# Four column-quarter matmuls of a state sum, recorded as one operation of a planned kernel

## The chip, the core and the metric

The kernel runs on one core of a Trainium2 chip. The metric is the device time of one execution in microseconds, taken as the median of several runs. One execution was also recorded by the hardware profiler; its instructions, waits and DMA packets are what the views below are made of.

## What is computed

The input is 4 sequences of 1024 tokens with 256 features, in f32 throughout. Four parts follow each other, each in a normalised residual form, `x = x + layernorm(part(layernorm(x)))`:

1. an encoder of 4 layers (linear attention with 16 heads, then a feed-forward part 256 to 1024 to 256),
2. a gated low-rank layer,
3. a state-space layer, over chunks of 512 tokens: projections, a short convolution, and then, for 512 channels with 16 states each, the recurrence

```
h = h * dA + (d * u) * b          # for every channel and state, along the tokens
y = sum over states of h * c      # the state sum
```

4. eight experts, each token sent to one of them, each expert with room for 320 tokens.

The change concerns the last line of part 3, the sum over states.

## The kernel before

**Blocks.** The 4096 tokens are 8 blocks of 512 (`NBLK`), and block `j` is half `j % 2` of a sequence. The encoder runs over units (sequence, layer, block) in a software pipeline. The state-space layer runs over the blocks: `front(j)` makes projections and the step sizes and stores them to memory, `scan(j)` does the recurrence and the state sum, `back(j)` projects and normalises, `route(j)` chooses experts. `experts` runs the expert matmuls, beside scans 6 and 7.

**The scan.** A chunk of 128 partitions holds 16 channels of 8 states, so a block of 128 channels (`db`, four of them) is 8 groups, and 16 states are two halves (`k` = 0 and 1, `NSH` = 2). The groups are visited as two rounds (`r`) of four quarters (`q`). For each `(q, k)` of a round: DMAs bring the step sizes (`dd`), GpSimd multiplies them with `b` (`dbu`), ScalarE makes the decay into PSUM (`h`), VectorE runs `tensor_tensor_scan` in place and then multiplies with `c` into a tile `hc`. There are 8 buffers for `hc`, as many as one round makes. In the blocks 0 to 4 GpSimd adds the two halves (`hc` of `k` = 1 takes the sum), so that only that one is summed by TensorE; in the blocks 5 to 7 both are.

**The state sum.** `sums(tiles, r, k)` issues four matmuls, one for each quarter `q`: the stationary operand is a 128x32 matrix of ones (`gsum`), the moving one is the 128x512 `hc` of that quarter, and the output is a quarter of the 128 partitions of the PSUM tile `y`. `y` has one buffer. The sums of a round are recorded one after the first tiles of the round that follows (list `late`), or at the end of `db`. At the end VectorE reads `y` into `ys` and the next `db` begins. Over the kernel there are 5x4x2 + 3x4x2x2 = 88 such calls, or 352 matmuls.

**The planner.** Nothing is emitted in the order of the program text. Every call is recorded as an operation (`record`, then `add`) with its buffers, a time for which it holds its engine (`busy`) and a time to its result (`done`). `order` is a list scheduler: of all operations whose inputs are ready and whose buffers can be placed, it takes the one that can start first by these costs, and at equal times the one recorded first. It also hands out the buffers: a tile's buffer comes free when its last user has been placed in the order. The result is one fixed order for each engine; on the chip every engine works through its own order and waits where an input isn't there. The cost that `record` gives to a TensorE matmul is

```
busy = 0.877 * n if out.shape[0] == 32 else 1.754 * max(n, 64) + (34 if n < P else 4)
```

so a quarter of a state sum (32 output rows, `n` = 512) is planned at 449 ns, and four of them at 1796 ns.

How much scan work is recorded between two pieces of the encoder is set by `pump` with `SSM_RATE`, and by fixed costs in the generators; none of this depends on the planner's costs.

All of this is recorded through a helper, so that nearly every instruction in the profile has line 203; groups are told apart by the names of their tiles.

Of the kernel before, what the change touches and what calls it, by code (L numbers as in the profile page):

```python
# [39 lines left out]
NSH = N_STATE // SH  # L40
# [4 lines left out]
GQ = 32 // GC  # L45
# [101 lines left out]
OVERLAP = {"vector": 84, "scalar": 99, "gpsimd": 42}  # L147
HANDOVER = 36
ISSUE, SCATTER, FIND = 350, 1700, 1500

LANES = 8
LATENCY, LANDING, BYTES_PER_NS = 1300, 700, 270.0
# [10 lines left out]
def columns(x):  # L163
    return math.prod(x.shape[1:])


class Program:
# [23 lines left out]
    def record(self, engine, name, args, kwargs):  # L191
        out = kwargs["out"] if "out" in kwargs else args[0]
        outs = [out] + [kwargs[k] for k in ("accum_out",) if k in kwargs]
        every = list(args) + list(kwargs.values())
        ins = [a for a in every if a is not out and (isinstance(a, View) or hasattr(a, "tensor"))]
        if kwargs.get("start") is False:
            ins.append(out)

        def emit():
            def put(a):  # L200
                return a.place() if isinstance(a, View) else a

            getattr(getattr(self.nc, engine), name)(  # L203
                *map(put, args), **{k: put(v) for k, v in kwargs.items()}
            )

        n, load = columns(out), 0
        if "dma" in name:
            src = kwargs["in_"] if "in_" in kwargs else args[1]
            small = out if isinstance(out, View) else src  # L210
            load = 4 * math.prod(small.shape) / BYTES_PER_NS
            busy = done = ISSUE
        elif name == "transpose":
            busy, done = 0.877 * n + 22, 320
        elif engine == "tensor":
            done = 1.754 * n + 190
            busy = 0.877 * n if out.shape[0] == 32 else 1.754 * max(n, 64) + (34 if n < P else 4)
        else:
            table = {"vector": VECTOR_NS, "scalar": SCALAR_NS, "gpsimd": GPSIMD_NS}[engine]
            a, b = table[name]  # L220
            if name in ("tensor_reduce", "bn_stats"):
                n = columns(ins[0])
            done = a + b * n
            if engine == "scalar":
                done += 60 * sum(isinstance(kwargs.get(k), View) for k in ("scale", "bias", "accum_out"))
            busy = max(done - OVERLAP[engine], 50)
        return self.add(engine, emit, outs, ins, busy, done, load)

    def add(self, engine, emit, outs, ins, busy, done, load=0):
        op = Op(engine, emit, outs, ins, busy, done, load)  # L230
        before = set()
        for write, aps in ((False, ins), (True, outs)):
            for a in aps:
                self.access(op, a, write, before)
        before.discard(op)
        for b in before:
            b.after.append(op)
        op.before = len(before)
        op.rank = len(self.ops)
        self.ops.append(op)  # L240
        return op
# [119 lines left out]
    def emit(self):  # L361
        with self.tc.manual_schedule():
            for op in self.order():
                op.emit()
        self.reset()
# [21 lines left out]
def sandwich_kernel(ctx: ExitStack, tc: tile.TileContext, io: dict):  # L387
    nc = tc.nc
    x_in, out = io["x"], io["out"]
# [37 lines left out]
    nc = Program(tc)  # L427
# [121 lines left out]
    def layers(ctx: ExitStack):  # L549
# [436 lines left out]
        m = {}  # L986
# [176 lines left out]
        def scan(j):  # L1163

            half = j % NB
            BC = []
            for side in range(2):
                t = fpool.tile([P, NSH, TB], F32, tag=f"bc{side}", name=f"bc{side}")
                nc.sync.dma_start(
                    t, bcd[j][side].unsqueeze(0).to_broadcast([GC, SH, NSH, TB])  # L1170
                )
                BC.append(t)
            Bt, Ct = BC
            begun.append(j)
            ys = Y[j] = fpool.tile([P, NDB, TB], F32, tag="ys", name="ys")
            for db in range(NDB):
                y = ps_y.tile([P, TB], F32, tag="y", name="y")

                def sums(tiles, r, k):
                    for q in range(4):  # L1180
                        nc.tensor.matmul(
                            y[q * 32 : (q + 1) * 32, :],
                            m["gsum"][:, r, :],
                            tiles[q, k],
                            start=r == 0 and k == first[r],
                            stop=r == GQ - 1 and k == NSH - 1,
                        )


                first = [NSH - 1 if j < NBLK - 3 else 0 for r in range(GQ)]  # L1190

                late = []
                for r in range(GQ):
                    if r == GQ // 2:
                        xl = fpool.tile([P, TB], F32, tag="xl", name="xl")
                        nc.sync.dma_start(xl, xcd[j][db])
                        zl = fpool.tile([P, TB], F32, tag="zl", name="zl")
                        nc.sync.dma_start(zl, zsd[j][db])
                    tiles = {}
                    for q in range(4):  # L1200
                        g = q * GQ + r
                        gg = db * (P // GC) + g
                        dd = []
                        for k in range(2):
                            t = spool.tile([P, TB], F32, tag=f"dd{k}", name=f"dd{k}", bufs=3)
                            nc.sync.dma_start(
                                t,
                                dud[j][db][g * GC : (g + 1) * GC, k, :].unsqueeze(1).to_broadcast([GC, SH, TB]),
                            )
                            dd.append(t)  # L1210
                        for k in range(NSH):
                            dbu = spool.tile([P, TB], F32, tag="dbu", name="dbu", bufs=3)
                            nc.gpsimd.tensor_tensor(dbu, dd[1], Bt[:, k, :], ALU.mult)
                            h = ps_h.tile([P, TB], F32, tag="h", name="h")
                            nc.scalar.activation(
                                h, dd[0], AF.Exp, scale=m["A"][:, gg, k : k + 1]
                            )
                            last = m["last_h"][:, gg, k : k + 1]
                            nc.vector.tensor_tensor_scan(
                                h, h, dbu, 0.0 if half == 0 else last, ALU.mult, ALU.add  # L1220
                            )
                            if half < NB - 1:
                                nc.vector.tensor_copy(last, h[:, TB - 1 : TB])
                            hc = tiles[q, k] = spool.tile([P, TB], F32, tag="hc", name="hc", bufs=8)
                            nc.vector.tensor_tensor(hc, h, Ct[:, k, :], ALU.mult)
                            if late:
                                sums(*late.pop(0))
                        if first[r]:
                            nc.gpsimd.tensor_tensor(hc, tiles[q, 0], hc, ALU.add)
                        yield 4  # L1230
                    late = [(tiles, r, k) for k in range(first[r], NSH)]
                for args in late:
                    sums(*args)
                t = ys[:, db, :]
                nc.vector.scalar_tensor_tensor(
                    t, xl, m["mcol"][:, db, M_D : M_D + 1], y, ALU.mult, ALU.add
                )
                nc.gpsimd.tensor_tensor(t, t, zl, ALU.mult)
                yield 0.8
# [586 lines left out]
```

## Time and profile before

| | us |
|---|---|
| median of 3 runs | 2791.13 (2789.11 to 2801.9) |
| the profiled execution, its time | 2787.44 |
| the profiled execution, its span from first to last instruction | 2785.7 |
| PE (TensorE matmul) busy | 2378.6 (85%) |
| DVE (VectorE) busy | 1752.6 (63%) |
| ACT (ScalarE) busy | 1591.2 (57%) |
| POOL (GpSimd) busy | 1527.6 (55%) |
| mean granted TensorE clock | 0.92 |

PE is matmul time, PEld the loading of stationary operands, which overlaps it. A matmul of f32 stands in the records as two, so a matmul of the program is two records ("x2"), and one state sum of four quarters is eight. Busy time of a group of records is the time in which at least one of them runs; records that run at the same time count once. The granted clock (PEclk) is a share of full speed. A wait is named as waiter and releaser: "PE y <- DVE hc" is TensorE idle ahead of a `y` matmul until a VectorE instruction that writes `hc` has ended. The chain of waits is the chain of work that ended last, followed backwards.

The execution has four stretches. Up to about 800 us there is only the encoder. From there to about 1890 us the encoder runs beside the scans 0 to 3. To about 2320 us its last units run beside the scans 4 and 5; about 100 us without a scan follow, in which the last encoder block is finished and projected. From 2420 us the scans 6 and 7 run beside the experts, and the last block is finished.

### The profile page before, as it was taken

What the parts mean: (1) busy time and instruction counts of PE and PEld (TensorE: products, weight loads), DVE (VectorE), ACT (ScalarE), POOL (GpSimd) and SP (SyncE); (2) the same over time, 40 slices, a digit from 0 to 9 for tenths busy, and PEclk for the clock granted to TensorE, in tenths of its full rate; (3) what the DMA queues carried; (4) which work ended last, traced back from release to release, by engine and by line L of the source; (5) the groups of instructions that cost most, each with busy time, mean ns of one, the idle gap of its engine ahead of it and who ended that gap; (6) DMA issues with size and microseconds to landing.
All of it is one profiled execution on the core that took longest, in us unless ns stands there. A gap on an engine that the chain in (4) does not pass through costs nothing.

```text
span 2785.7 us, 29116 instructions
## 1 busy us (share of the span) xinstructions
PE 2378.6 (85%) x8308; PEld 1380.3 (50%) x8308; DVE 1752.6 (63%) x3291; ACT 1591.2 (57%) x3309; POOL 1527.6 (55%) x2005
## 2 busy tenths in 40 slices
PE   4889699998999999997989899986986975799776
PEld 2555456655555555555645555643443543344343
DVE  2121232223468878884449978896897894599895
ACT  4434454456676666664666766765665543666443
POOL 1101020123267667784429769885894773467774
PEclk8989899999999999999999999997897886899788
DMA  4011101112254344442245445445344352767762
GB/s 106 22 47 59 59 25 35 54 51 79 95 167 134 118 143 140 148 126 87 84 143 171 135 133 188 159 144 167 126 153 152 117 168 73 234 200 231 206 172 61
DMA packets 202218, 342.01 MB, mean 123 GB/s; under 512 B 32198, under 2 KB 79515, under 8 KB 198977
## 3 DMA queue, kind: packets, MB, share of 16 engines
q1 hardware_dynamic: 197760, 334.80, 38.3%
q0 software_dynamic: 4288, 5.27, 1.0%
q8 instruction: 68, 1.11, 0.2%
q14 instruction: 102, 0.83, 0.1%
HBM read 281.13 MB, written 59.92 MB: 122 GB/s over the span
## 4 chain that ended last, share of the span: by engine, by line
PE 41%; DVE 20%; POOL 14%; ACT 14%; issue 8%; DMA 3%; SPq 0%; POOLq 0%; DVEq 0%; ACTq 0%
PE mm L203 36%; DVE h L203 7%; ACT tok L203 6%; POOL dbu L203 5%; DVE hc L203 3%; PE kv L203 2%; PE y L203 2%; POOL tok L203 2%; POOL hc L203 2%; DVE st L203 2%; DVE xc L203 2%; POOL t L203 2%; ACT h L203 2%; DVE kv L203 1%; ACT t L203 1%
## 5 line engine op out<-in xcount | busy, mean ns | idle before, releaser
L203 POOL TENSOR_TENSOR dbu<-dd,bc 128x512 f32<-128x512 f32 x512 | 663.0, 1333 | 147.8 <-DVE h L203 104.5
L203 ACT ACTIVATE h<-dd,A 128x512 f32<-128x512 f32 x512 | 344.8, 687 | 317.7 <-DVE hc L203 304.1
L203 PE MATMUL mm<-w,fT 128*128 128x256 f32 x2176 | 486.6, 381 | 6.1 <-ACT t L203 2.7
L203 PEld LDWEIGHTS mm<-w,fT 128*128 128x128 f32 x2176 | 410.2, 190 | 86.6 <-issue 18.9
L203 DVE TENSOR_TENSOR_SCAN h<-h,last_h,dbu 128x512 f32<-128x512 f32 x256 | 321.6, 1279 | 62.2 <-ACT h L203 40.3
L203 DVE TENSOR_TENSOR hc<-h,bc 128x512 f32<-128x512 f32 x512 | 341.6, 678 | 9.8 <-PE y L203 8.1
L203 DVE TENSOR_TENSOR_SCAN h<-h,dbu 128x512 f32<-128x512 f32 x256 | 305.6, 1219 | 42.9 <-ACT h L203 33.0
L203 PE MATMUL y<-hc,gsum 128*32 128x512 f32 x704 | 222.2, 664 | 84.0 <-DVE hc L203 57.6
L203 PE MATMUL mm<-hT,w1a 128*128 128x512 f32 (+1 forms) x576 | 269.0, 617 | 14.8 <-ACT hT L203 11.0
L203 PE MATMUL mm<-hT,w1b 128*128 128x512 f32 (+1 forms) x576 | 251.2, 583 | 12.8 <-ACT fT L203 6.2
L203 POOL TENSOR_TENSOR hc<-hc,hc 128x512 f32<-128x512 f32 x160 | 213.8, 1336 | 52.6 <-DVE hc L203 46.8
L203 PE MATMUL mm<-wkv,hT 128*128 128x512 f32 x512 | 228.2, 597 | 1.5 <-ACT xi L203 0.8
L203 ACT ACTIVATE fT<-mm,cols 128x512 f32<-128x512 f32 x256 | 170.8, 682 | 85.5 <-PE mm L203 84.8
L203 PE MATMUL mm<-ident,tok 128*128 128x128 f32 x696 | 114.0, 306 | 107.9 <-ACT tok L203 105.9
L203 POOL TENSOR_SCALAR ve<-mv 128x4 f32<-128x4 f32 (+1 forms) x105 | 20.7, 197 | 335.1 <-DVE mv L203 323.0
L203 DVE TENSOR_TENSOR X<-X,mm 128x512 f32<-128x512 f32 x128 | 86.7, 679 | 169.8 <-PE mm L203 169.5
L203 POOL TENSOR_TENSOR X<-X,ro 128x1024 f32<-128x1024 f32 x64 | 151.3, 2367 | 68.3 <-ACT tok L203 48.4
L203 PEld LDWEIGHTS mm<-hT,w1a 128*128 128x128 f32 x576 | 113.0, 205 | 147.9 <-issue 97.6
L203 PEld LDWEIGHTS mm<-hT,w1b 128*128 128x128 f32 x576 | 107.5, 191 | 152.2 <-issue 102.4
L203 ACT ACTIVATE tok<-X,nb,rs 128x256 f32<-128x256 f32 x288 | 149.3, 589 | 43.3 <-POOL nb L203 42.7
L203 PEld LDWEIGHTS mm<-ident,tok 128*128 128x128 f32 x696 | 86.6, 154 | 164.6 <-ACT tok L203 127.7
L203 ACT ACTIVATE tok<-tok,nb,rs 128x256 f32<-128x256 f32 x252 | 131.3, 589 | 60.8 <-POOL nb L203 58.4
(194 smaller groups left out, 3925.6 us busy)
## 6 DMA issues: line engine op xcount, KB each, us to landing
dd<-dud SPq DMA_DIRECT2D x512, 256.0 KB
w<-in_w_dram SPq DMA_DIRECT2D x16, 1024.0 KB
dud<-t SPq DMA_DIRECT2D x32, 512.0 KB
tok<-in_x_dram SPq DMA_DIRECT2D x16, 512.0 KB
wkv<-in_wkv_dram SPq DMA_DIRECT2D x16, 512.0 KB
w1a<-in_w_dram SPq DMA_DIRECT2D x16, 512.0 KB
w1b<-in_w_dram SPq DMA_DIRECT2D x16, 512.0 KB
t<-in_w_in_dram SPq DMA_DIRECT2D x16, 512.0 KB
```

What stands on the lines that cost most here:

```text
L203: getattr(getattr(self.nc, engine), name)(*map(put, args), **{k: put(v) for k, v in kwargs.items()})
```

## The change

The four matmuls of a call of `sums` become one operation for the planner, which emits them one behind the other. The operation has all four quarters as inputs, so it is placed when all four `hc` tiles are ready, and their buffers come free together, when it is done. Its planned cost is 1.754x512 + 100 = 998 ns of the engine, and 1198 ns to the result. The matmuls themselves, their operands and their number are the same. The planner's order is made anew with these costs, so instructions of all engines may move.

```
+SIDE = 100
...
+    def side_by_side(self, calls):
+
+        outs, ins = [], []
+        for out, lhsT, rhs, start, stop in calls:
+            outs.append(out)
+            ins += [lhsT, rhs] + ([] if start else [out])
+
+        def emit():
+            for *views, start, stop in calls:
+                self.nc.tensor.matmul(
+                    *(v.place() if isinstance(v, View) else v for v in views), start=start, stop=stop
+                )
+
+        n = columns(calls[0][0])
+        return self.add("tensor", emit, outs, ins, 1.754 * n + SIDE, 1.754 * n + 300)
...
                 def sums(tiles, r, k):
-                    for q in range(4):
-                        nc.tensor.matmul(
-                            y[q * 32 : (q + 1) * 32, :],
-                            m["gsum"][:, r, :],
-                            tiles[q, k],
-                            start=r == 0 and k == first[r],
-                            stop=r == GQ - 1 and k == NSH - 1,
-                        )
+                    start = r == 0 and k == first[r]
+                    stop = r == GQ - 1 and k == NSH - 1
+                    nc.side_by_side(
+                        [
+                            (y[q * 32 : (q + 1) * 32, :], m["gsum"][:, r, :], tiles[q, k], start, stop)
+                            for q in range(4)
+                        ]
+                    )
```

In the built order of the kernel before, the 352 matmuls of `y` stand on TensorE in 144 runs without another instruction between them: 73 of one matmul, 24 of two, 9 of three, 17 of four and 21 longer ones. In that of the changed kernel they stand in 74 runs: 61 of four, 12 of eight and one of twelve.

## The prediction

> **What bounds the kernel.** I read the page first, then the windows by stage, all engines and then the tile `y` alone, then the timeline of TensorE around single state sums, then the waits and the chain.
>
> ```profile
> PE 2378.6 (85%) x8308; PEld 1380.3 (50%) x8308; DVE 1752.6 (63%) x3291; ACT 1591.2 (57%) x3309; POOL 1527.6 (55%) x2005
> L203 PE MATMUL y<-hc,gsum 128*32 128x512 f32 x704 | 222.2, 664 | 84.0 <-DVE hc L203 57.6
> ```
>
> TensorE is the busiest engine, and the state sums are 222.2 us of its 2378.6: 9% of it, 8% of the span. 704 records of 664 ns would be 467 us one after the other, so many already overlap.
>
> ```profile
> core 0: us, PE busy (x) PEld busy (x) DVE busy (x) ACT busy (x) POOL busy (x), PEclk, DMA share, GB/s
> 770.00:1890.00 1120.00, 1029.46 (x3701) 608.66 (x3701) 852.95 (x1553) 736.41 (x1498) 793.06 (x979) 0.97 0.44 138
> 1890.00:2320.00 430.00, 337.32 (x1106) 176.81 (x1105) 349.19 (x651) 242.17 (x459) 315.40 (x360) 0.85 0.46 144
> 2420.00:2786.00 366.00, 297.85 (x1062) 151.76 (x1060) 304.10 (x487) 191.93 (x428) 248.00 (x270) 0.89 0.62 179
> ```
>
> I call these stages A, B and D. In A TensorE is busy 92% of the time and no other engine over 76%: TensorE bounds it. In B and D VectorE is at 81% and 83%, level with TensorE or ahead of it. The tile `y` alone, in the same windows:
>
> ```profile
> core 0: us, PE busy (x) PEld busy (x) DVE busy (x), PEclk, DMA share, GB/s
> 770.00:1890.00 1120.00, 69.94 (x254) 9.43 (x254) 11.03 (x15) 0.97 0.44 138
> 1890.00:2320.00 430.00, 68.95 (x194) 9.15 (x194) 6.68 (x9) 0.85 0.46 144
> 2420.00:2786.00 366.00, 83.29 (x256) 12.50 (x256) 5.84 (x8) 0.89 0.62 179
> ```
>
> The timeline of TensorE shows what a state sum costs alone and in company (start, length, records):
>
> ```profile
> 1229.07 1.07 PE L203 MATMUL y<-hc,gsum 128*32 128x512 f32 x8
> 1242.93 1.04 PE L203 MATMUL y<-hc,gsum 128*32 128x512 f32 x2
> ...
> 2442.31 1.90 PE L203 MATMUL y<-hc,gsum 128*32 128x512 f32 x10
> 2447.90 1.04 PE L203 MATMUL y<-hc,gsum 128*32 128x512 f32 x2 [0.69 <-DVE hc L203]
> ...
> 2618.37 1.91 PE L203 MATMUL y<-hc,gsum 128*32 128x512 f32 x2 [4.15 <-DVE hc L203]
> 2622.55 1.92 PE L203 MATMUL y<-hc,gsum 128*32 128x512 f32 x2 [2.27 <-DVE hc L203]
> ```
>
> Four quarters in one run take 1.07 us, one quarter alone 1.04: the four run side by side, and a single pays for all. In D each round has three singles of `k` = 0 as their tiles appear, and at its end a run of five (the last quarter of `k` = 0 and the four of `k` = 1) in 1.90 us. At the low clock of an idle stretch a single takes 1.9.
>
> The chain of waits, finally, in the windows 770 to 1330, 1890 to 2320 and 2420 to 2786:
>
> ```profile
> by line: PE mm L203 29.3%; POOL dbu L203 9.7%; DVE h L203 7.1%; issue 6.7%; ACT tok L203 6.5%; POOL X L203 3.6%; POOL hc L203 3.6%; DVE hc L203 3.1%; POOL tok L203 2.7%; DVE kv L203 2.5%; DVE st L203 2.0%; ACT h L203 1.9%; PE y L203 1.6%; P
> ...
> by line: PE mm L203 15.8%; issue 13.5%; DVE h L203 11.3%; POOL dbu L203 9.8%; PE y L203 5.7%; DVE hc L203 4.4%; POOL hc L203 3.1%; ACT t L203 2.5%; DVE st L203 2.4%; ACT tok L203 2.4%; DVE xc L203 2.3%; POOL tok L203 2.2%; ACT h L203 2.1%;
> ...
> by line: PE mm L203 24.8%; issue 13.3%; DVE h L203 13.3%; PE y L203 6.3%; DVE hc L203 5.9%; PE kv L203 4.7%; DMA out_dram<-X,own 4.5%; ACT h L203 4.3%; POOL dbu L203 3.8%; ACT tok L203 1.9%; ACT X L203 1.7%; POOL t L203 1.6%; DVE own L203 1
> ```
>
> The page gives `PE y` 2.3% of it, or 64 us. By these windows it is 1.6% of 560 us, 5.7% of 430 in B, and 6.3% of 366 in D: 9.0, 24.5 and 23.1; what is left, 7.5, is the rest of A. So of the sums' busy time 16.5 of 70 us lie on the chain in A (24%), 24.5 of 69 in B (36%), 23.1 of 83 in D (28%).
>
> **The change, part by part.** *Sums in A.* Scans 0 to 3 have 32 calls; at 1.07 us they take 34 us instead of 70: 36 us of TensorE saved. Upper bound: a stage bound by TensorE gets all 36. Lower: only the chain's share counts, 24% of 36, or 9. I take 20, between the two: the encoder's own matmuls behind the sums on TensorE start earlier too (they lead the chain in both halves of A, with 29% and 25%), but TensorE's idle 90 us in A show that handovers with other engines set part of the pace.
>
> *Sums in B.* 24 calls, at 1.07 to 1.92 us by clock; at about 1.5 they are 36 us instead of 69, so 33 saved, 36% of it on the chain: 12. Lower bound 0, where VectorE (81%) holds the pace. I take 6.
>
> *Sums in D.* 32 calls. Two calls in a row cost what a run of five costs now, 1.90; so the round's end stays as it is, and only the three singles a round go. With some at the lower clock I put 1.1 us a call, 36 us instead of 83; of the 47 saved 28% is on the chain: 13. Lower bound 0, since scans 6 and 7 are VectorE's to pace. I take 5: the experts' matmuls gain room, but the scan must still be run through.
>
> *The new wait.* A call now starts when its fourth tile is there. What lies behind it on TensorE's queue is encoder or expert matmuls; the planner puts them ahead of the call where they are ready, and three separate stops of TensorE for VectorE become one. "PE y <- DVE hc" is 57.6 us in all now; I count nothing for less of it, since an early matmul gained the sum nothing: its end waited for the last quarter anyway.
>
> *Buffers held longer.* A round fills all eight `hc` buffers in blocks 5 to 7. Before, the first came free with the first single, long before the next round needed it; now with the first call, at the round's end. VectorE is covered by two scans of 1.17 us each between the last `hc` of a round and the next one (a row of VectorE at 2444.86 has them at 2.34). A call of 1.05 us fits if TensorE comes to it at once. I went through the 24 rounds: where does the round's last quarter of `k` = 0 start, plus 1.1, against the start of the next round's first `hc`? It would be late in five: by 7.5 us near 2230 (sums at 2237.00, `hc` at 2230.60), by 16 near 2710 (sums at 2724.65, `hc` at about 2709.6), by 1.1, 1.0 and 0.5 in the others, 26 us together. These are bounds from the order of before:
>
> ```profile
> 2719.63 0.16 DVE L203 SCALAR_TENSOR_TENSOR pp<-ex,pp 128x3 f32<-128x3 f32 x1 [6.63 <-ACT X L203]
> 2720.26 0.69 DVE L203 TENSOR_TENSOR hc<-h,bc 128x512 f32<-128x512 f32 x1 [0.47 <-PE y L203]
> ```
>
> Near 2710 VectorE stands still for an expert anyway (6.63 us), so most of that 16 is no new loss. I take 7 (0 to 26). In blocks 0 to 4 four buffers are free of it, and cover the next two quarters: nothing.
>
> *The rest of the order.* All engines' orders change. In both built orders the scans begin and end beside the same encoder units, so the interleaving stays. I take 0 for it and have no row to size it; it is in the chances.
>
> *Clock.* TensorE runs at 0.89 in D now, and the single at 2618.37, after 4.15 us idle, ran at the low clock; so did the next, so singles of this spacing don't hold it up. I count nothing.
>
> The Trainium skill ("TensorE: Matmul & The Clock Gate", "What's actually happening") speaks against the change here: an idle window of about 3.4 us halves the clock, so taking away singles that break up idle time should cost matmuls around them. If by that rule D fell to about 0.80, its 215 us of other matmul would take some 24 more, a quarter of it on the chain, and the sum would be smaller by 6.
>
> **Sum.** 20 + 6 + 5 - 7 = 24 us less. The profiled execution would come from 2787.4 to 2763.4; the median of the runs lies 3.7 above it, so 2767. Bounds: at best 36 + 12 + 13 = 61 less (2730), at worst 9 less and 26 more (2808).
>
> **Rivals.** *The room is not used.* TensorE's saving in A turns into idle time: POOL `dbu` (9.7% of the chain from 770 to 1330) and VectorE's scans keep the pace, and B and D give nothing. Then A's 9 less against the 7 of the buffers: 2789. For it: of the chain in A only some 30% is TensorE. Against: 92% busy over 1120 us leaves little else to explain that stretch.
>
> *VectorE waits for the buffers.* In rounds of blocks 5 to 7, wherever TensorE comes to the first call more than about 2.3 us after the round's last `hc`, the next round's `hc` waits, and with it scans, GpSimd and the DMAs behind them. If B and D pay the full 26 and A gives 9, it is 2791 + 17 = 2808. For it: "DVE hc <- PE y" is there already, 8.1 us in 4 waits. Against: in scan 6 the sums begin within 1 us of their tile in nearly every round, and no stall would appear there.
>
> *The change does nothing*, the calls being split again: excluded, since the built order has all runs in fours. That a run of four takes one matmul's time is a row of before.
>
> **Chances.** The forecast 0.60, room not used 0.20, buffers 0.20. A measurement of this kernel can tell about 0.5% from no change, 14 us. Forecast and its better end give faster 0.60; the first rival is same, 0.20; the second slower, 0.20, with what a worse order may cost. Range: from 2738, leaving out the last 8 us of the best bound, to 2808, where the second rival stands.
>
> **What would show it.** `y` busy falls from 222 to about 105 us, at about 1.06 for eight records. Stage A (first `hc` of scan 0 at 810 to last of scan 3 at 1888) is 15 to 35 us shorter, with TensorE still near 92%. Scans 6 and 7 keep their 158 and 163 us. "DVE hc <- PE y" grows from 8.1 to under 20. Wrong if A keeps its length while TensorE's idle time grows (first rival), if "DVE hc <- PE y" grows beyond 25 us (second), or if the gain or loss lies where no sum runs.

## The result and the profile after

No difference: 2792.74 us (median, 2785.82 to 2799.68) against 2791.48 (2788.08 to 2801.9) beside it; ratio 0.9999, interval 0.9987 to 1.0012. The profiled execution of the changed kernel took 2795.6 us, with a span of 2793.8. The page's lines for TensorE and the sums:

```profile
PE 2325.1 (83%) x8308; PEld 1385.7 (50%) x8308; DVE 1767.0 (63%) x3291; ACT 1592.9 (57%) x3309; POOL 1528.2 (55%) x2005
L239 PE MATMUL y<-hc,gsum 128*32 128x512 f32 x704 | 130.4, 666 | 40.8 <-DVE hc L204 34.9
```

The change did what it says: the sums went from 222.2 to 130.4 us of TensorE, and the four quarters of a call run side by side, in eight records, with parts of a call standing alone only where TensorE has to wait inside it. Where the clock is low they take longer: the two calls at 2631.29, after 12.84 us of idle time and one group of other matmuls, take 4.82 us (start, length, records, on the timeline of TensorE):

```profile
1237.84 1.07 PE L239 MATMUL y<-hc,gsum 128*32 128x512 f32 x8
...
2440.99 1.06 PE L239 MATMUL y<-hc,gsum 128*32 128x512 f32 x8
...
2614.64 1.92 PE L239 MATMUL y<-hc,gsum 128*32 128x512 f32 x2 [2.06 <-DVE hc L204]
...
2631.29 4.82 PE L239 MATMUL y<-hc,gsum 128*32 128x512 f32 x16
```

The stages A, B and D again, first all engines, then `y` alone:

```profile
770.00:1890.00 1120.00, 1009.69 (x3686) 612.03 (x3684) 848.61 (x1541) 730.67 (x1488) 790.11 (x976) 0.95 0.44 137
1890.00:2320.00 430.00, 316.74 (x1124) 175.79 (x1125) 362.67 (x664) 246.31 (x463) 316.80 (x357) 0.82 0.47 147
2420.00:2786.00 366.00, 282.42 (x1066) 154.30 (x1064) 309.16 (x486) 192.55 (x428) 249.49 (x270) 0.85 0.62 178
...
770.00:1890.00 1120.00, 36.05 (x248) 5.32 (x248) 11.04 (x15) 0.95 0.44 137
1890.00:2320.00 430.00, 38.06 (x200) 5.83 (x200) 6.66 (x9) 0.82 0.47 147
2420.00:2786.00 366.00, 56.28 (x256) 8.47 (x256) 5.88 (x8) 0.85 0.62 178
```

In A the sums lost 34 us, as forecast (69.94 to 36.05), but TensorE as a whole only 20 (1029.46 to 1009.69): the other matmuls took 14 more, at a granted clock of 0.95 instead of 0.97. The 20 became idle time, most of it ahead of encoder matmuls. The waits of TensorE in the window 770 to 1890, before and after (us in total, times, longest):

```profile
PE kv L203 <- DVE kv L203: 21.7, 8, 5.3
PE mm L203 <- ACT tok L203: 12.6, 3, 10.5
PE mm L203 <- ACT t L203: 10.4, 11, 2.7
PE mm L203 <- ACT hT L203: 4.8, 4, 2.3
```

```profile
PE mm L204 <- ACT tok L204: 22.5, 6, 9.8
PE mm L204 <- ACT t L204: 16.7, 15, 3.4
PE mm L204 <- ACT hT L204: 14.7, 10, 3.6
PE kv L204 <- DVE kv L204: 10.3, 8, 4.8
```

TensorE now waits longer for ScalarE ahead of the encoder's matmuls: 12.6 to 22.5 for `tok`, 10.4 to 16.7 for `t`, 4.8 to 14.7 for `hT`. Below, stretches are counted by the scans, so that they can be compared between kernels: A from the first `hc` of scan 0 to the last of scan 3, B to the end of scan 5, D from the start of scan 6 to the end of the last `ys`. Before they are 1078, 424 and 336 us; after 1087, 411 and 341: A and D, where a gain was forecast too, are longer, and B is shorter by 13. Each length is of one execution, the profiled one.

### The profile page after: what moved, and what is told of

Its sections match the earlier page's. It is cut to its first block, busy times and chain, and to the rows that moved or that the text cites. A ratio compares the mean times of both kernels' runs of the same rounds, so it can differ in the third digit from the quotient of the medians.

```text
span 2793.8 us, 29101 instructions
## 1 busy us (share of the span) xinstructions
PE 2325.1 (83%) x8308; PEld 1385.7 (50%) x8308; DVE 1767.0 (63%) x3291; ACT 1592.9 (57%) x3309; POOL 1528.2 (55%) x2005
## 5 line engine op out<-in xcount | busy, mean ns | idle before, releaser
L204 PE MATMUL mm<-hT,w1a 128*128 128x512 f32 (+1 forms) x576 | 276.9, 630 | 30.0 <-ACT hT L204 21.7
L204 PE MATMUL mm<-ident,tok 128*128 128x128 f32 x696 | 116.3, 310 | 141.9 <-ACT tok L204 139.9
L239 PE MATMUL y<-hc,gsum 128*32 128x512 f32 x704 | 130.4, 666 | 40.8 <-DVE hc L204 34.9
```

The costliest lines, as they stand in the source:

```text
L204: getattr(getattr(self.nc, engine), name)(*map(put, args), **{k: put(v) for k, v in kwargs.items()})
L239: self.nc.tensor.matmul(*(v.place() if isinstance(v, View) else v for v in views), start=start, stop=stop)
```

## The experiments

Three theories for the missing gain. *Order*: the planner's new order gave it back. *Clock*: less TensorE work lowers the granted clock, and the other matmuls take the time. *Handover* (the prediction's first rival, widened): the sums' time lies off the path, which runs through chains over several engines. The expectations also call the last one the room theory. In each experiment the list order of all other engines is that of its parent, unless said otherwise: only what an operation emits is changed, not what it is planned at.

**The order of before, sums grouped at emission.**

```
+            order = self.order()
+            waiting = []
...
+                if quarter is not None:
+                    waiting.append(op)
+                    if quarter == 3:
+                        flush()
+                    continue
```

> The order of the kernel before on every engine, made with its old costs; only at emission the single sums are held back and issued together at the place of the fourth (39 runs of four, 18 of eight, and 15 broken ones where a tile's buffer would be written again first). No other instruction moves. If the new order gave back the gain (order theory): the grouping alone is worth most of what was forecast, 15 to 25 us, so about 2770 where before is 2791. If TensorE's room isn't used (room theory): within 6 us of before, with y busy near 135 us instead of 222 and TensorE's idle time larger by as much. If the clock takes it back (clock theory): also within 6 us of before, but with the granted clock at about 0.905 instead of 0.92 and the other matmuls' busy time some 30 us longer than before.

Measured: 2794.31 us, ratio to before 0.9994 (0.9985 to 1.0004). `y` busy 139.9 us, clock 0.908, other matmuls 2190 us up to the last `ys` (2168 before). The order theory falls: with every other instruction in its old place, 82 us less of sums are worth at most 4 us by the interval. Handover and clock both said this.

**Only the last call of each block of channels.**

```
             for *views, start, stop in calls:
-                self.nc.tensor.matmul(
-                    *(v.place() if isinstance(v, View) else v for v in views), start=start, stop=stop
-                )
+                if stop:
+                    self.nc.tensor.matmul(
+                        *(v.place() if isinstance(v, View) else v for v in views), start=True, stop=stop
+                    )
```

> The order of the changed kernel on every engine, but of its 88 calls only the 32 last ones of each block of channels are issued; the other 56 are left out of the state sum. Nothing else moves. y busy falls from 130 to about 45 us. Order theory (TensorE's time is worth something in a given order): 20 to 40 us faster than the changed kernel. Room theory: within 8 us of it, the idle time of TensorE growing by some 80. Clock theory: within 8 us too, the granted clock falling to 0.89 or less and the other matmuls taking 20 us more.

The altered sums change where tokens go, and the kernel's branch for tokens that find no place ran after the main part (3011.67 us in all), so it is read up to the end of the last `ys`: 2762 us, against 2767 in the changed kernel. 82 us less of `y` (130.4 to 48.9) brought 5. The clock up to there is 0.897, against 0.907 in the changed kernel, and the other matmuls take 10 us more; the clock theory had 0.89 or less and 20. So the handover theory's 8 holds, the order theory's 20 to 40 doesn't, and the clock took back a part.

**Every call twice.**

> The order of the changed kernel, every call issued twice in a row with halved ones, so that the sum is the same; one small VectorE instruction more at the start. y busy doubles from 130 to about 230 to 260 us, as much as before or more. Order theory: 30 to 60 us slower than the changed kernel. Room theory: at most 15 us slower. Clock theory: at most 15 us slower, the granted clock back at about 0.92 and the other matmuls 25 us or more shorter.

2809.3 us, ratio 1.0048 (1.0033 to 1.0064); `y` 207 us, below the expected 230 to 260; the last `ys` ends at 2783, 16 later than in the changed kernel. The slope is a fifth: 16 us for 77. That is at the edge of the handover theory's 15 (by the ratios of the medians it is 14), and far from the order theory's 30 to 60. So 77 us more of sums cost 16, where 82 us less gained 5. The clock came back to 0.914 and the other matmuls to 2176, 21 us less, not the 25 of the clock theory.

**Planned at the old total.**

```
-        return self.add("tensor", emit, outs, ins, 1.754 * n + SIDE, 1.754 * n + 300)
+        return self.add("tensor", emit, outs, ins, 4 * 0.877 * n, 3 * 0.877 * n + 1.754 * n + 190)
```

> The changed kernel, but its one operation is planned at the old total, 1796 ns, so a third order comes out. Order theory: orders differ in what they are worth, so it lies apart from the changed kernel by over 10 us, to either side. Room and clock theories: within 8 us of before and of the changed kernel.

2798.53 us, ratio 1.0004 (0.9992 to 1.0016): a third order, the same time.

**What is A's pace, then?** Four runs take work away from one engine at a time, in the order of the changed kernel. Each leaves out the emission of some operations (`op.emit = lambda: None`), and each was executed once.

> The order of the changed kernel, but the second half of the contraction of the feed-forward's first matmul is left out (256 of 512 matmuls of w1a and w1b), so TensorE has about 240 us less to do in the whole, some 115 us of it between the start of scan 0 and the end of scan 3 (stretch A, 1087 us in the changed kernel). Read by stretches, up to the last ys. TensorE theory (A is bound by TensorE; the sums' time was merely beside it): A shorter by 80 us or more. Handover theory (A is paced by chains through ScalarE and VectorE, in whose queues the scan's work stands): A shorter by less than 60. The stretch before scan 0, 813 us and without sums, should lose some 70 of its 120 in both.

> The order of the changed kernel, but the VectorE scan of the second half of the states is left out (248 instructions of 1.25 us, some 310 us of VectorE, about 145 in A); the state after it is what stood there. TensorE theory: A within 20 us of 1087. Handover theory: A shorter by 40 us or more. The last stretch (scan 6 to the last ys, 341 us) should fall by 50 or more in both, as VectorE paces it.

> As the run without the second half's scans, and the ScalarE exponentials of that half are left out as well (248 of 0.69 us, 170 us of ScalarE, some 85 in A). TensorE theory: A within 20 us of the changed kernel. Handover theory: a further 20 us or more off A, since norms and exponentials share ScalarE's queue.

> The order of the changed kernel, but GpSimd's product dbu is left out for the second half of the states (248 of 1.33 us, 330 us of GpSimd, some 160 in A); the scan reads what stood there. TensorE theory: A within 20 us. Handover theory: A shorter by 20 to 60 us, since GpSimd also works in the norms (ve, t, nb) of the encoder, which stand behind dbu in its queue.

| left out | engine, us in A (estimate) | its busy time in A fell by | A, 1087 with nothing left out | gained |
|---|---|---|---|---|
| half the contraction of w1a, w1b | TensorE 115 | 73 | 1078 | 9 |
| half the scans | VectorE 145 | 120 | 1072 | 15 |
| the same and their exponentials | with ScalarE 85 | 121, ScalarE 71 | 1065 | 22 |
| half of `dbu` | GpSimd 160 | 148 | 1056 | 31 |
| 56 of 88 sums | TensorE 18 | 10 | 1088 | 0 |

For the first row, A in the changed kernel and then in this run, its ends rounded to whole microseconds:

```profile
813.00:1900.00 1087.00, 977.98 (x3575) 591.34 (x3574) 840.44 (x1514) 709.40 (x1443) 770.56 (x945) 0.95 0.43 136
```

```profile
781.00:1860.00 1079.00, 906.04 (x3319) 553.30 (x3318) 837.21 (x1514) 708.04 (x1444) 773.13 (x947) 0.92 0.43 138
```

TensorE is busy 90% of A, and leaving out a tenth of A's length in matmuls gains 9 us. So the TensorE theory falls by its own number (80 or more). Of the handover theory's numbers the one for GpSimd holds (20 to 60, measured 31), while those for VectorE and ScalarE are too large (40 and a further 20, measured 15 and a further 7): no engine's work returns much more than a fifth. What the runs show is that no single engine sets A's pace; that it is the fixed order, five queues waiting for each other in turn, is the reading that remains, not one that a run isolates. A run that takes work off TensorE and GpSimd at once is missing. In the first row a part of the saving also came back as slower matmuls: TensorE's busy time fell by some 73 us, not 115, with the clock at 0.92 instead of 0.95. Before scan 0, where the encoder is alone, the same run lost 32 us (813 to 781) where some 70 were expected, for 66 us less of TensorE's busy time: half comes back there, an eighth in A. The last stretch fell by 3, 9, 16 and 14 us in the four runs, so VectorE alone doesn't pace D either; I had expected 50 from half the scans.

**The clock, held up.** Idle-time matmuls, read by nobody, are put on TensorE ahead of the instructions before which the kernel's own profile shows idle time.

```
+                if op.engine == "tensor" and self.fill:
+                    n = FILL.get(at, 0)
+                    spare = self.places["ps_kv", "kv"].tiles[0][:, 384:512] if n else None
+                    for _ in range(n):
+                        self.nc.tensor.matmul(spare, self.ident, self.ident, start=False, stop=False, ...)
```

> The changed kernel in its own order, with 1017 small idle-time matmuls (128x128, ident by ident, into spare columns of the kv bank, read by nobody) put on TensorE ahead of the 120 instructions before which its profile shows over 0.8 us of idle time, for three quarters of that time each. They keep TensorE busy, so its clock should be granted nearly throughout (over 0.96 instead of 0.905) and the other matmuls lose some 60 us or more of busy time against 2197. Clock theory (the saved time came back as slower matmuls): the changed kernel with fill is 15 us or more faster than the kernel before with fill. Handover theory (the sums' time lies off the path, and the clock too): the two with fill are within 8 us of each other, and each within 15 us of its own kernel.

> The kernel before in its own order, with 854 such idle-time matmuls ahead of the 108 instructions before which its profile shows over 0.8 us of idle time. The partner of the changed kernel with fill: clock theory 15 us or more slower than that one, handover theory within 8 us of it.

2759.19 us for the changed kernel (0.9865, 0.9843 to 0.9887), 2745.96 for the one before (0.9823, 0.9803 to 0.9843). The other matmuls, up to the last `ys`, took 2130 us instead of 2197 and 2106 instead of 2168. Both theories missed: the clock is worth time (32 and 46 us), which the handover theory denied, and the changed kernel isn't ahead by 15 but behind by 13, which the clock theory denied. But the changed kernel's clock was 0.95 and its partner's 0.973, so a denser fill followed, for three kernels by one rule; the grouped one has the order of before.

> The kernel before with a denser fill: idle-time matmuls for nine tenths of each idle time over 0.4 us in its own profile (1118 in 164 places). The partner of the next two. Its clock should be at 0.975 or above and its time near the first fill's 2746, within 12 us.

> The order of the kernel before with the sums grouped at emission (as in the run with the old plan), and the same fill rule by that run's profile (1316 in 173 places). All other engines stand as in its partner. If the sums' saved time was worth something and only the falling clock took it back (clock theory): 10 us or more faster than the partner with single sums. If the sums lie off the path (handover theory): within 6 us of it, y busy some 70 us smaller.

> The changed kernel in its own order with the same fill rule (1316 in 176 places). Clock theory: as fast as the partner with single sums or 10 us faster, since its clock now is held up as well. Handover theory: within 10 us of the grouped run in the old order; what differs is what the new order is worth.

Single sums in the old order: 2730.73 (0.9762, 0.9740 to 0.9784), clock 0.985, and 15 us below the first fill, where within 12 was expected. Grouped in the old order: 2758.03 (0.9857, 0.9835 to 0.9878). The changed kernel: 2745.12 (0.9818, 0.9797 to 0.9838). Both theories missed again: the grouped run is 27 us behind its partner, which neither had, and the changed kernel is 13 us from the grouped run and 14 behind the single one. So the runs are read by stretches. First the stretch A of the single and of the grouped run, all engines, then `y`:

```profile
786.00:1860.00 1074.00, 1037.08 (x4075) 638.31 (x4074) 837.10 (x1514) 709.38 (x1445) 770.00 (x946) 0.99 0.44 138
...
786.00:1860.00 1074.00, 68.16 (x254) 9.34 (x254) 11.01 (x15) 0.99 0.44 138
```

```profile
788.00:1860.00 1072.00, 1027.22 (x4178) 648.92 (x4177) 834.37 (x1513) 711.17 (x1447) 770.79 (x947) 0.99 0.44 138
...
788.00:1860.00 1072.00, 43.26 (x248) 6.22 (x248) 11.00 (x15) 0.99 0.44 138
```

The order and the clock of 0.99 are the same, `y` takes 68 and 43 us, and A lasts 1074 and 1072. TensorE as a whole has only 10 us less to do, since the fill rule put 13 us more of idle-time matmuls into the grouped run's A. They can hardly have taken the gain back: after 35 of their 41 groups in A TensorE still stands idle. In three runs below, with the same orders and the same two fills in A, it lasts 1073.3 us with single sums, and 1071.1 and 1073.4 with grouped ones. So 25 us of sums are worth 1 to 2 us in A, on the mean of these five executions: they lie off its path, and the clock isn't what hid their worth.

Most of the loss of 27 us lay in D (331 against 357 us), where "DVE hc <- PE y" rose from 5.7 to 17.4 us. That looked like the prediction's second rival, the `hc` buffers held too long. A run that groups the blocks 0 to 4 alone, with the single run beside it again:

> The order of the kernel before, the sums grouped at emission in the blocks 0 to 4 alone and single in the blocks 5 to 7, with the fill of the grouped run up to block 4 and that of the single run after it. If holding the hc buffers of the last blocks is what cost the grouped run its 27 us (buffer theory): within 8 us of the single run at about 2731, the last stretch back at about 332 us from 357, 'DVE hc <- PE y' there back under 8 us. If grouping costs in another way: 2745 or more. If grouped sums are worth something where no buffer is short: 8 us or more faster than the single run.

> The single run with fill again, beside the one above: 2731, within 8 us.

2730.53 (0.9773, 0.9757 to 0.9790) against 2729.38 (0.9777, 0.9761 to 0.9793): grouping in the blocks 0 to 4 is worth nothing, as found for A. That D is back at 332 seemed to confirm the buffers, but this run has the single run's fill in D as well, so two things changed at once. The grouped run's own timelines, TensorE's and then VectorE's, show another cause:

```profile
2577.20 12.53 PE L376 MATMUL kv<-ident 128*128 128x128 f32 x86 [14.26 <-ACT X L205]
...
2590.67 1.06 PE L205 MATMUL y<-hc,gsum 128*32 128x512 f32 x6
```

```profile
2591.75 0.69 DVE L205 TENSOR_TENSOR hc<-h,bc 128x512 f32<-128x512 f32 x1 [7.00 <-PE y L205]
```

The idle-time matmuls at 2577 waited 14.26 us themselves, since an expert's ScalarE work still read the bank that they write to, and then ran for 12.53 ahead of real work. The wait is the kernel's own: grouped without fill, TensorE waits 13.10 us there, ahead of an expert's `kv` matmul. What was meant to fill it could start only at its end. The sum behind them was late, and VectorE with it. The first fill of the changed kernel has the same at 2594 (a wait of 12.9), its denser fill at 2580, so those two times are spoilt in D by the experiment itself. Without five such groups:

> The grouped run in the order of before with fill, without the five groups of idle-time matmuls (75 of 1316) that waited over 2 us for the kv bank in the last stretch. If the loss was theirs: 2725 to 2742, the last stretch near 335 us, 'DVE hc <- PE y' there under 9 us; the single run with fill is at 2730. If the hc buffers cost it (buffer theory): 2745 or more, the last stretch still above 345, 'DVE hc <- PE y' still over 12 us. If grouping is worth something at full clock: under 2722.

2740.79 us (0.9794, 0.9775 to 0.9813). D is 337 us and "DVE hc <- PE y" 6.9: the loss was mostly the fill's, and the buffers are not shown to cost anything beyond the unclear rest. That rest, 10 us against the single runs, stays open: it is spread over B (407 against 403), D (337 against 331) and the stretches before each of them, and the clock in D is not the same, 0.94 against 0.98. A part of it can still be the fill's, for two more groups in D waited for the bank, 2.89 and 4.74 us, and then ran for 2.50 and 5.36. No run shows a gain from grouping: in D 27 us less of `y` (75.59 to 48.35) come with no shorter stretch.

**Another balance.** More or less scan work beside the encoder (a planner constant; the order is made anew).

> The changed kernel with SSM_RATE (31, 31, 38) instead of (34, 34, 42): less scan work recorded between two pieces of the encoder. If TensorE had room that a new balance could use, one of the two rates would be over 10 us faster than the changed kernel. Handover theory: both within 15 us, neither faster by over 8.

> The changed kernel with SSM_RATE (37, 37, 46): more scan work recorded between two pieces of the encoder. Expected as for the lower rate: over 10 us faster if the room can be used by balance, within 15 us and not faster by over 8 by the handover theory.

2823.37 us (1.0101, 1.0083 to 1.0120) and 2802.99 (1.0037, 1.0023 to 1.0050): both slower than before and than the changed kernel, the lower rate by some 30 us, more than the 15 expected. At these two rates the freed time isn't used.

**A version that beats both** came out of the fill: single sums, old order, idle time filled, 2730 us, 2.2% to 2.4% faster than before.

## Why the prediction was wrong

The forecast was 24 us off, 2767. The measured time lies in the range but shows no change; the first rival, the room that isn't used, had 2789 and a chance of 0.20. Its sign is what came: A kept its length (1078 and 1087 us) while TensorE's idle time in it grew from 86 to 109. Its reason is not borne out: leaving out half of `dbu` or half the scans took 31 and 15 us off A, so neither of the two keeps the pace alone. By the steps of the prediction:

- *The size of the saving* was right in A (36 forecast, 34 measured) and in B (33 and 31), and wrong in D: 47 forecast, 27 measured. The 32 calls there take 56 us, 1.76 each instead of 1.1, since some run at the low clock after idle time and some are broken by waits inside them. So `y` fell to 130 us, not to about 105.
- *Sums in A, 20 us*, is the step that failed. It took a point between the chain's share (9) and the whole saving (36), because 92% busy seemed to leave little else to explain the stretch. In the old order, 28 us less of sums left A at 1081 us instead of 1078; at an equal clock, 25 us less were worth 1 to 2. Even the lower bound was too high. That the chain of waits is one path among near-equal ones, and that time taken off it alone brings out the next, is a reading that fits this. TensorE's own work fits it too: some 115 us of matmuls in A were worth 9.
- *Sums in B, 6, and in D, 5*, are not shown. Without fill, B is 419 us in the old order with grouped sums and 411 in the changed kernel, instead of 424; with fill it is 409 and 407 grouped against 403 and 404 single. D is 344 and 341 instead of 336 without fill. All are single executions, and B's sign changes, so no gain can be told.
- *Clock, nothing*: wrong by a term that was there. The sums' 92 us less came with 29 us more for the other matmuls (2168 to 2197 up to the last `ys`) and 0.904 instead of 0.92. The Trainium skill's clock rule, weighed at 6 us against the change, had the direction that this case then showed; its size in D was smaller than was worked out from it, 0.86 and 6 us more of other matmuls, not 0.80 and 24. It isn't why the gain is missing, though: in A it is missing at 0.99 too.
- *Buffers, 7*: "DVE hc <- PE y" went from 8.1 to 9.8 us, so 2. The second rival, 26 us, did not happen.
- *The rest of the order, 0*: right for the whole, as three orders lie within 0.1% of each other by their ratios. By stretches A grew by 9 us and D by 5 while B shrank by 13, so that they cancel is partly luck.

## What to carry to other kernels

A busy share of 92% doesn't show that an engine bounds a stretch when several in-order queues wait for each other: the test is to leave out some of its work in the same order and see what comes back, and here about a tenth came back. A share of the chain of waits was no lower bound of what a saving is worth: 9 us by it, 1 to 2 measured. Where a profile shows the clock below full, keeping TensorE busy in its idle time may be worth more than shortening its matmuls, as it was here.

## What the runs showed of the hardware

Filling TensorE's idle time with matmuls that nobody reads made the kernel 2.4% faster (0.9762), with more work on the engine. The kernel's own matmuls other than the sums took 2082 us instead of 2168, up to the last `ys`. The stretches of before and of the single run with the denser fill, cut at the start of scan 0 and the ends of scans 3 and 5, the start of scan 6 and the last `ys`:

```profile
0.00:810.00 810.00, 693.76 (x2406) 433.00 (x2407) 224.88 (x528) 398.29 (x881) 158.69 (x369) 0.93 0.20 63
810.00:1888.00 1078.00, 992.09 (x3577) 585.95 (x3576) 834.68 (x1512) 708.11 (x1442) 770.75 (x947) 0.97 0.43 137
1888.00:2312.00 424.00, 333.50 (x1098) 174.82 (x1100) 346.73 (x640) 241.37 (x456) 314.46 (x356) 0.85 0.47 146
2312.00:2425.00 113.00, 66.42 (x193) 38.21 (x186) 45.84 (x132) 53.30 (x108) 40.65 (x71) 0.71 0.48 148
2425.00:2761.00 336.00, 288.26 (x1023) 144.59 (x1021) 291.02 (x459) 184.10 (x408) 234.02 (x237) 0.90 0.65 189
```

```profile
0.00:786.00 786.00, 733.99 (x3009) 488.09 (x3010) 224.41 (x527) 398.19 (x880) 158.82 (x369) 0.99 0.21 64
786.00:1860.00 1074.00, 1037.08 (x4075) 638.31 (x4074) 837.10 (x1514) 709.38 (x1445) 770.00 (x946) 0.99 0.44 138
1860.00:2263.00 403.00, 369.15 (x1654) 229.19 (x1652) 346.60 (x640) 239.82 (x453) 315.06 (x355) 0.98 0.50 154
2263.00:2369.00 106.00, 92.85 (x486) 70.54 (x483) 47.16 (x132) 53.23 (x108) 40.07 (x70) 0.90 0.48 154
2369.00:2701.00 332.00, 308.16 (x1304) 173.69 (x1303) 293.16 (x460) 183.82 (x408) 235.75 (x238) 0.98 0.66 193
```

The gain lies where the encoder runs alone (24 us), in B (21) and between the scans (7); in A and D it is 4 each. The Trainium skill ("TensorE: Matmul & The Clock Gate", "What's actually happening") names the mechanism, a clock that follows how busy TensorE was a few microseconds ago. These rows agree with it: with TensorE busier, the clock is 0.99 instead of 0.93 before scan 0, and 0.98 instead of 0.85 in B; how far back it looks they don't show.
